# A graph network with per-node sorting: three groups of tiles instead of five, one buffer for each, and min and max as scalar_tensor_tensor

## The chip, the cores and the metric

The kernel runs on one core of a Trainium2 chip. The metric is the device time of one execution in microseconds (us); before the change it is 3176.69 us, the median of 3 runs (3176.14 to 3177.83).

## The reference, cut to what matters

Four graph layers run over x (16 graphs, 1024 nodes, 64 channels) with a sparse weighted adjacency (16 x 1024 x 1024, some 16 neighbours per node). Each layer ends in a layer norm over the residual. Layer 1 is the one that the change touches: for each node, some neighbours are dropped by a rule on their rank, and then, for each channel, three quantiles of the remaining neighbours' values are taken and summed with weights.

```python
# layer 1, for each graph; valid is the diluted adjacency > 0
vals = jnp.where(valid[..., None], x[:, None, :, :], big)
sv = jnp.sort(vals, axis=2)               # sort over the neighbours
for tau, wt in zip((0.25, 0.5, 0.75), (0.25, 0.5, 0.25)):
    pos = tau * (m - 1)                   # m valid neighbours
    agg += wt * (sv[floor(pos)] * (1 - frac) + sv[ceil(pos)] * frac)
# then x = layernorm(x + mlp(x + agg))
```

Layer 0 is one adjacency product, layer 2 is three of them with 128 channels, layer 3 is one with a threshold.

## The kernel before

**Tiling.** The 1024 nodes of a graph are ranked by their number of kept neighbours and permuted, so that each tile of 128 nodes holds nodes of like degree. `KS` gives the slots of the eight tiles: 31, 21, 19, 17, 15, 15, 13, 11. A slot holds one neighbour's row: R = 66 floats, 64 channels and 2 columns with the numbers of that neighbour's dropped partners. Tiles with like counts are sorted together, as a group (`GROUPS`): tile 0 alone with 31 slots, tiles 6 and 7 with 13, tiles 2 and 3 with 19, tiles 4 and 5 with 15, tile 1 alone with 21.

**The stages of a graph**, each a Python generator that emits a few instructions at a time:
- `words_of` (L502) reads the adjacency in 8 rows of tiles, transposes them on TensorE, makes bit words, runs layer 0 and stores the transposed adjacency to DRAM.
- `front` and `listing` (L555, L587) turn the words into neighbour lists `idx` and write the table of rows to DRAM.
- `gathered` (L808) fetches a group's rows. Each slot of 128 nodes is one indirect DMA issued by GpSimd (L815); short slots of two tiles share one through `PACKS` and `stage`. That is 129 per graph: 122 whole slots and 7 packs.
- `masked` (L847) marks dropped neighbours: VectorE finds them for one tile at a time (L862, L864), ScalarE adds a large bias to each slot (L868), and the weights `hat` of the ranks come from ScalarE (L886, L887). It needs a tile's gathers to have landed.
- `quantiles` (L891) sorts: a hand-made sorting network `NETS[n]` of min and max over whole runs of slots, each one `tensor_tensor` on VectorE (L906), between the gathered buffer `g` and a second buffer `s`.
- `summed` (L916) scales the ranks that can carry weight (`RANKS`) on ScalarE (L932), one instruction for each rank and tile, and adds them up on TensorE through an identity matrix (L936).
- `back` (L1122) does the rest of layer 1 and layers 2 and 3.

**Buffers.** All groups share four `g` buffers (tag "x", L813) and two `s` buffers (tag "y", L896), each large enough for the largest group.

**What sets the order.** Nothing is reordered by a scheduler. The loop at L1249 gives every generator a start in planned microseconds and a stretch; a heap (L1267) then emits their steps by planned time, the 16 graphs overlapping. So each engine's queue is fixed at build time, and an engine that reaches an instruction whose input is late waits there with all that stands behind it. `LENGTHS` are the planned lengths of the five sorts, 192.06 us in all for a graph; `WORDS`, `LISTS` and `BACK` stretch the other stages.

```python
add(start(q - 2), gathered(st, g), (start(q - 1) - start(q - 2)) / (many + 1))
half = (start(q) - start(q - 1)) * (PAIRS if len(GROUPS[g]) > 1 else MASKS)
add(start(q) - half, masked(st, g), 0.9 * half / (1.5 + 0.4 * count + 2.1 * len(GROUPS[g])))
add(start(q), quantiles(st, g), (start(q + 1) - start(q)) / (cost + 0.1))
add(start(q + 1) + SUMS, summed(st, g))
```

Of the kernel before, what the change touches and what calls it, by code (L numbers as in the profile page):

```python
# [10 lines left out]
F32 = mybir.dt.float32  # L11
# [9 lines left out]
P = 128  # L21
# [8 lines left out]
GROUPS = ((0,), (6, 7), (2, 3), (4, 5), (1,))  # L30
# [21 lines left out]
LENGTHS = (50.06, 35, 54.5, 19.5, 33)  # L52
WORDS, LISTS, BACK = 152.6, 133.2, 178
WORDS_STEPS, LISTS_STEPS, BACK_STEPS = 82.0, 74.0, 181.0
BEFORE = 7.874
# [10 lines left out]
RANKS = {13: (0, 9), 15: (2, 11), 19: (2, 14), 21: (3, 15), 31: (4, 23)}  # L66
# [6 lines left out]
    13: (  # L73
        "2,0,1,0,1,2,2,2,6;3,0,1,1,1,2,2,2,6;12,0,2,0,2,4,4,4,3;15,0,2,2,2,4,4,4,3;6,1,2,1,1,"
        "4,4,4,3;7,1,2,2,1,4,4,4,3;2,0,4,0,1,8,8,8,2;3,0,4,4,1,8,8,8,2;13,3,7,7,1,0,0,0,1;14,"
        "3,7,3,1,0,0,0,1;13,0,8,8,1,1,-3,-3,2;14,0,8,0,1,1,-3,1,2;13,2,6,6,1,8,6,6,2;14,2,6,2"
        ",1,8,6,8,2;12,2,4,2,1,7,6,7,2;13,2,4,4,1,7,6,6,2;11,3,5,5,1,8,7,7,2;10,3,5,3,1,8,7,8"
        ",2;8,1,2,1,1,2,2,2,3;9,1,2,2,1,2,2,2,3;2,1,9,1,2,0,0,0,1;1,1,9,9,2,0,0,0,1;5,3,11,11"
        ",2,0,0,0,1;4,3,11,3,2,0,0,0,1;3,4,8,8,3,0,0,0,1;0,4,8,4,4,0,0,0,1;11,2,4,4,1,8,8,8,1"
        ";10,2,4,2,1,8,8,8,2;2,3,5,3,1,0,0,0,1;3,3,5,5,1,0,0,0,1;6,6,8,6,2,0,0,0,1;7,6,8,8,2,"  # L80
        "0,0,0,1;12,1,2,1,1,2,2,2,5;13,1,2,2,1,2,2,2,4"
    ),
    15: (
        "3,0,1,1,1,2,2,2,7;0,0,1,0,1,2,2,2,7;3,0,2,2,1,4,4,4,4;0,0,2,0,1,4,4,4,4;13,1,3,3,1,4"
        ",4,4,3;14,1,3,1,1,4,4,4,3;12,1,2,1,1,4,4,4,4;13,1,2,2,1,4,4,4,4;3,0,4,4,3,8,8,8,2;0,"
        "0,4,0,3,8,8,8,2;3,3,7,7,1,0,0,0,1;0,3,7,3,1,0,0,0,1;6,2,4,2,2,8,8,8,2;5,2,4,4,2,8,8,"
        "8,2;5,1,2,2,1,4,4,4,4;4,1,2,1,1,4,4,4,4;8,3,4,3,1,8,8,8,2;9,3,4,4,1,8,8,8,2;2,1,9,1,"
        "6,0,0,0,1;1,0,8,8,6,0,0,0,1;8,4,8,4,4,0,0,0,1;9,4,8,8,4,0,0,0,1;11,2,4,4,2,0,0,0,1;1"
        "0,2,4,2,2,0,0,0,1;2,6,8,6,2,4,4,4,2;3,6,8,8,2,4,4,4,2;12,3,4,3,1,2,2,2,5;13,1,2,2,1,"
        "2,2,2,5"  # L90
    ),
    19: (
        "2,0,1,0,1,2,2,2,8;3,0,1,1,1,2,2,2,8;12,0,2,0,2,4,4,4,4;15,0,2,2,2,4,4,4,4;5,1,2,2,1,"
        "4,4,4,4;4,1,2,1,1,4,4,4,4;2,0,4,0,3,8,8,8,2;3,0,4,4,3,8,8,8,2;13,3,7,7,1,8,8,8,2;14,"
        "3,7,3,1,8,8,8,2;12,2,4,2,2,8,8,8,2;15,2,4,4,2,8,8,8,2;6,3,4,3,1,8,8,8,2;7,3,4,4,1,8,"
        "8,8,2;12,0,8,0,1,4,4,4,2;13,0,8,8,1,4,4,4,2;12,5,6,5,1,8,8,8,2;13,5,6,6,1,8,8,8,2;11"
        ",1,2,2,1,8,8,8,2;10,1,2,1,1,8,8,8,2;3,5,13,13,2,0,0,0,1;0,5,13,5,3,0,0,0,1;3,4,8,8,1"
        ",12,9,9,2;0,4,8,4,1,12,9,12,2;12,1,9,1,3,0,0,0,1;15,1,9,9,3,0,0,0,1;2,2,4,2,1,14,14,"
        "14,2;1,2,4,4,1,14,14,14,2;6,5,9,5,3,0,0,0,1;7,5,9,9,3,0,0,0,1;5,1,2,2,1,0,0,0,1;4,1,"
        "2,1,1,0,0,0,1;12,6,8,6,2,0,0,0,1;15,6,8,8,2,0,0,0,1;11,10,12,12,1,7,6,6,2;10,10,12,1"  # L100
        "0,1,7,6,7,2;5,0,16,16,3,0,0,0,1;4,1,17,1,2,0,0,0,1;5,3,5,5,1,4,3,3,2;4,3,5,3,1,4,3,4"
        ",2;12,9,10,9,1,2,3,2,2;13,9,10,10,1,2,3,3,2;2,8,16,8,3,0,0,0,1;3,8,16,16,3,0,0,0,1;2"
        ",3,4,3,1,2,2,2,2;3,3,4,4,1,2,2,2,2;6,11,12,11,1,2,2,2,2;7,11,12,12,1,2,2,2,2;12,4,8,"
        "4,3,8,8,8,2;13,4,8,8,3,8,8,8,2;2,2,4,2,1,4,4,4,4;3,2,4,4,1,4,4,4,3;2,7,9,7,1,0,0,0,1"
        ";3,7,9,9,1,0,0,0,1;11,3,5,5,1,8,8,8,2;10,3,5,3,1,8,8,8,2;5,1,2,2,1,0,0,0,1;12,3,4,3,"
        "1,2,2,2,6;13,3,4,4,1,2,2,2,6"
    ),
    21: (
        "2,0,1,0,1,2,2,2,8;1,0,1,1,1,2,2,2,8;13,0,2,2,1,4,4,4,4;14,0,2,0,1,4,4,4,4;3,1,3,3,1,"
        "4,4,4,4;0,1,3,1,1,4,4,4,4;2,1,2,1,1,4,4,4,4;3,1,2,2,1,4,4,4,4;12,0,4,0,4,8,8,8,2;13,"  # L110
        "0,4,4,4,8,8,8,2;2,2,4,2,2,8,8,8,2;3,2,4,4,2,8,8,8,2;5,1,2,2,1,8,8,8,2;4,1,2,1,1,8,8,"
        "8,2;12,3,4,3,1,8,8,8,2;13,3,4,4,1,8,8,8,2;8,5,6,5,1,8,8,8,2;9,5,6,6,1,8,8,8,2;3,18,1"
        "9,19,1,0,0,0,1;0,18,19,18,1,0,0,0,1;2,0,8,0,2,4,4,4,2;3,0,8,8,2,4,4,4,2;2,16,17,16,1"
        ",4,1,4,2;3,16,17,17,1,4,1,1,2;12,4,8,4,2,0,0,0,1;15,4,8,8,2,0,0,0,1;12,16,20,16,1,3,"
        "-2,3,2;15,16,20,20,1,3,-2,-2,2;2,2,10,2,2,4,4,4,2;1,2,10,10,2,4,4,4,2;11,2,4,4,2,4,6"
        ",6,2;10,2,4,2,2,4,6,4,2;11,17,19,19,1,0,0,0,1;10,17,19,17,1,0,0,0,1;12,18,20,18,1,0,"
        "0,0,1;13,18,20,20,1,0,0,0,1;12,6,8,6,2,4,4,4,2;13,6,8,8,2,4,4,4,2;12,1,2,1,1,2,2,2,2"
        ";13,1,2,2,1,2,2,2,2;11,17,18,18,1,2,2,2,2;10,17,18,17,1,2,2,2,2;9,0,16,16,1,0,0,0,1;"
        "5,1,17,17,4,0,0,0,1;4,2,18,2,3,0,0,0,1;2,7,8,7,1,2,2,2,3;3,7,8,8,1,2,2,2,3;11,8,16,1"
        "6,4,0,0,0,1;10,8,16,8,5,0,0,0,1;11,5,6,6,1,0,0,0,1;10,5,6,5,1,0,0,0,1;2,13,14,13,1,0"  # L120
# [1195 lines left out]
```

## Time and profile before

| what | value |
|---|---|
| median of 3 runs | 3176.69 us |
| span of the profiled execution, first to last instruction | 4328.2 us |
| share of its chain of waits on "another core or an unknown queue" | 28.0% |
| VectorE (DVE) busy, instructions | 2822.0 us, 6935 |
| GpSimd (POOL) busy, instructions | 2160.8 us, 2078 |
| TensorE (PE) busy, instructions | 2647.8 us, 13765 |
| ScalarE (ACT) busy, instructions | 1914.0 us, 6153 |
| the sort, L906 | 3648 instructions, 228 for each graph |
| mean granted TensorE clock | 0.764 |

The page gives no other time for the profiled execution than its span, and the span is 1151 us longer than the median of the runs. Busy time is the union of an engine's instructions. A group's row gives line, engine, operation, tiles and shapes, count, then busy us and mean ns of one, then the idle time of its engine just before such instructions and what ended it. Since the order is fixed at build time, each engine ran the same instructions in the same order in the profiled execution as in the timed ones, and only the waits between them can differ.

### The profile page before, as it was taken

The numbers are of one execution on the slowest core, as the hardware profiler recorded it, in microseconds if no ns is written. First come the engines' busy times: TensorE is split into PE (matmuls) and PEld (weight loads), VectorE is DVE, ScalarE is ACT, GpSimd is POOL, SyncE is SP. The second block draws the span as 40 slices with busy tenths as digits, with TensorE's granted clock in tenths as the row PEclk, the third lists the DMA queues.
The fourth block names the chain that finished last, engine by engine and source line by source line (L and its number), as shares of the span: only waits on it lengthen the run. The fifth ranks groups of instructions, "written<-read, shape, count | busy, mean of one in ns | idle before, by whom it ended". The sixth has DMA issues, their size and how long they took to land.

```text
span 4328.2 us, 46055 instructions
## 1 busy us (share of the span) xinstructions
PE 2647.8 (61%) x13765; PEld 1635.7 (38%) x13766; DVE 2822.0 (65%) x6935; ACT 1914.0 (44%) x6153; POOL 2160.8 (50%) x2078
## 2 busy tenths in 40 slices
PE   6034285675848567584755758476575848456478
PEld 5023152443525244352533435253343525233243
DVE  6058383865849486594857668485766859476671
ACT  2034352634536264453535455363545536253641
POOL 1715626455454645546465464546545554645600
PEclk8566597787969778796877879687787969768688
DMA  3212121322222132222213222231322222111210
GB/s 107 42 50 70 34 67 37 104 54 78 73 71 84 40 101 56 78 77 74 77 39 90 64 83 76 65 84 40 100 60 79 78 80 71 39 57 24 62 43 3
DMA packets 169056, 282.54 MB, mean 65 GB/s; under 512 B 99485, under 2 KB 102112, under 8 KB 166880
## 3 DMA queue, kind: packets, MB, share of 16 engines
q1 hardware_dynamic: 67584, 142.01, 9.9%
q0 software_dynamic: 66048, 69.88, 9.1%
q10 hardware_dynamic: 35168, 67.62, 4.1%
q8 instruction: 114, 1.87, 0.2%
q14 instruction: 142, 1.16, 0.1%
HBM read 204.33 MB, written 71.44 MB: 64 GB/s over the span
## 4 chain that ended last, share of the span: by engine, by line
another core or an unknown queue 28%; DVE 25%; PE 23%; ACT 16%; issue 7%; DMA 0%; ACTq 0%; DVEq 0%
DVE g L906 7%; PE mm L1207 7%; DVE s L906 7%; ACT g L868 6%; ACT ones_at L974 3%; PE ax L464 3%; ACT ones_at L975 2%; PE tp L439 2%; PE mm L377 2%; PE pa L936 2%; PE mm L1196 2%; ACT g L932 1%; PE mm L1141 1%; DVE top L707 1%
## 5 line engine op out<-in xcount | busy, mean ns | idle before, releaser
L815 POOL DMA_INDIRECT g<-table,idx x1952 | 2045.4, 1048 | 1919.7 <-PE pa L936 666.8
L1207 PE MATMUL mm<-adjB,msg 128*128 128x512 f32 x1536 | 769.6, 621 | 109.1 <-issue 82.4
L936 PE MATMUL pa<-g,ident 128*128 128x128 f32 (+1 forms) x1600 | 376.0, 360 | 430.1 <-ACT g L932 300.5
L868 ACT ACTIVATE g<-g,bias 128x64 f32<-128x64 f32 (+9 forms) x2272 | 596.8, 341 | 47.9 <-DVE bias L864 29.2
L906 DVE TENSOR_TENSOR s<-g 128x256 f32<-128x256 f32 (+9 forms) x944 | 531.3, 588 | 64.5 <-ACT g L868 55.5
L936 PEld LDWEIGHTS pa<-g,ident 128*128 128x128 f32 x1600 | 312.3, 248 | 574.0 <-ACT g L932 347.1
L906 DVE TENSOR_TENSOR g<-s 128x256 f32<-128x256 f32 (+8 forms) x864 | 473.4, 573 | 9.0 <-DVE s L906 3.0
L932 ACT ACTIVATE g<-g,w 128x64 f32<-128x64 f32 x1552 | 397.8, 341 | 17.2 <-DVE w L912 13.6
L1207 PEld LDWEIGHTS mm<-adjB,msg 128*128 128x128 f32 x1536 | 268.7, 197 | 301.1 <-issue 270.7
L1147 DVE TENSOR_TENSOR u<-mm,mb 128x512 f32<-128x512 f32 x32 | 22.1, 691 | 463.1 <-remote 313.5
L464 PE MATMUL ax<-at,xt 128*64 128x128 f32 x1920 | 284.5, 310 | 17.4 <-issue 17.4
L377 PE MATMUL mm<-adjB,x 128*64 128x512 f32 x512 | 272.6, 666 | 36.3 <-issue 31.3
L979 PE MATMUL mm<-ones_at,pieces 128*64 128x512 bf16 x768 | 213.0, 420 | 119.0 <-ACT ones_at L975 77.1
L464 PEld LDWEIGHTS ax<-at,xt 128*64 128x64 f32 x1920 | 250.2, 158 | 81.2 <-issue 79.1
L439 PE MATMUL tp<-ident,arow 128*128 128x128 f32 x1024 | 181.7, 309 | 156.2 <-remote 66.4
L399 DVE TENSOR_REDUCE ln_v<-sq 128x8 f32<-128x512 f32 x64 | 43.6, 681 | 296.4 <-issue 156.8
L439 PEld LDWEIGHTS tp<-ident,arow 128*128 128x128 f32 x1024 | 140.9, 162 | 205.1 <-issue 131.7
L441 ACT COPY at<-tp 128x512 f32<-128x512 f32 x240 | 139.0, 580 | 177.2 <-remote 122.3
L906 DVE TENSOR_TENSOR g<-g,s 128x256 f32<-128x256 f32 (+5 forms) x432 | 199.1, 464 | 15.1 <-remote 5.0
L906 DVE TENSOR_TENSOR g<-g 128x256 f32<-128x256 f32 (+8 forms) x304 | 200.7, 660 | 11.2 <-remote 4.0
L1219 PE MATMUL mm<-ident,tT 64*128 64x64 f32 x128 | 25.7, 295 | 293.9 <-ACT tT L380 207.4
L1210 ACT ACTIVATE hlT<-mm 128x512 f32<-128x512 f32 x96 | 57.4, 598 | 296.4 <-PE mm L1207 123.7
(225 smaller groups left out, 4361.9 us busy)
## 6 DMA issues: line engine op xcount, KB each, us to landing
arow<-in_adj_dram SPq DMA_DIRECT2D x128, 512.0 KB
adjd<-at ACTq DMA_DIRECT2D x120, 512.0 KB
adjB<-adjd SPq DMA_DIRECT2D x15, 4096.0 KB
g<-table,idx POOLq DMA_INDIRECT x1952
table<-xc ACTq DMA_DIRECT2D x16, 264.0 KB
xt<-in_x_dram SPq DMA_DIRECT2D x16, 256.0 KB
out_dram<-y SPq DMA_DIRECT2D x16, 256.0 KB
stage<-table,packed POOLq DMA_INDIRECT x112
```

What stands on the lines that cost most here:

```text
L377: nc.tensor.matmul(pa[:C, :], src[:, m, :], adjT[:, h * TH:(h + 1) * TH, m, :], start=(m == 0), stop=(m == T - 1))
L439: nc.tensor.transpose(pt[:, i * P:(i + 1) * P], a[:, j * P:(j + 1) * P], ident)
L441: nc.scalar.copy(at[:, h * TH:(h + 1) * TH, :], pt.rearrange("p (i n) -> p i n", n=P))
L464: nc.tensor.matmul(self.bank[:C, cols], self.xt[:, m + 1, :], at[:, m, :], start=(m == 0), stop=(m == T - 1))
L815: nc.gpsimd.indirect_dma_start(out=dst, out_offset=None, in_=st["table"], in_offset=bass.IndirectOffsetOnAxis(ap=index, axis=0))
L868: nc.scalar.activation(v, v, AF.Identity, bias=bias[:m, i, k:k + 1])
L906: nc.vector.tensor_tensor(box(bufs[mode >> 1 & 1], d, run, sd, count), box(bufs[mode >> 3], a, run, sa, count), box(bufs[mode >> 2 & 1], b ...
L932: nc.scalar.activation(slots(g, bufs[0], lo + r, lo + r + 1)[:, i, 0, :C], slots(g, bufs[at[r]], lo + r, lo + r + 1)[:, i, 0, :C], AF.Iden ...
L936: nc.tensor.matmul(pa[:, :(e - k) * nt * C], ident, rows_.rearrange("p (k c) -> p k c", c=R)[:, :, :C], start=(j == 0), stop=(j == len(run ...
L974: nc.scalar.activation(ones_at, iota, AF.Abs, bias=st["minus"][:, s:s + 1])
L979: nc.tensor.matmul(bank[:C, :], pieces[:, i, s, :], ones_at[:, h * HALF:(h + 1) * HALF], start=(s == 0 and i == 0), stop=False)
L1207: nc.tensor.matmul(pg, msg[:, m, :], adjT[:, h * TH:(h + 1) * TH, m, :], start=(m == 0), stop=(m == T - 1))
```

## The change

- Five groups become three: tile 0 (31 slots), tiles 4 to 7 (15 slots each), tiles 1 to 3 (21 slots each). The networks for 15 and 21 slots are new ones, those for 13 and 19 go. Smaller tiles are padded to the group's slots.
- Each group has one `g` buffer of its own (tags x0, x1, x2), and there is one `s` buffer. A group's gathers for the next graph are emitted only after its sum for this graph.
- Each min and max is a `scalar_tensor_tensor`: times 1.0, then min or max with the second tensor. Where a step has several runs (or a later step reads the columns), it takes all 66 columns of a slot as one contiguous run (`widths`), otherwise 64.
- `summed` handles ranks of three or four tiles with one matmul, 36 for each graph; ranks that a smaller tile cannot carry are left out for that tile.
- The plan has 176 us for a graph, and new constants `TURN` and `FREED`.

The networks' rows, the same renaming of tags in the fallback path, and unchanged context are cut from this diff.

```diff
-GROUPS = ((0,), (6, 7), (2, 3), (4, 5), (1,))
+GROUPS = ((0,), (4, 5, 6, 7), (1, 2, 3))
...
-LENGTHS = (50.06, 35, 54.5, 19.5, 33)
-WORDS, LISTS, BACK = 152.6, 133.2, 178
+LENGTHS = (46.0, 55.0, 75.0)
+WORDS, LISTS, BACK = 140.0, 122.0, 164.0
 WORDS_STEPS, LISTS_STEPS, BACK_STEPS = 82.0, 74.0, 181.0
-BEFORE = 7.874
+BEFORE = 8.0
+TURN = 90.0
+FREED = 20.0
...
-RANKS = {13: (0, 9), 15: (2, 11), 19: (2, 14), 21: (3, 15), 31: (4, 23)}
+RANKS = {11: (0, 9), 13: (0, 9), 15: (2, 11), 17: (2, 14), 19: (2, 14), 21: (3, 15), 31: (4, 23)}
...
+def widths(n, nt, narrow, full):
+
+    def places(buf, first, run, step, count):
+        return {(buf, first + i * step + r) for i in range(count) for r in range(run)}
+
+    read, found = set(), []
+    for mode, a, b, d, run, sa, sb, sd, count in reversed(network(n)):
+        out = places(mode >> 1 & 1, d, run, sd, count)
+        wide = bool(out & read) or (count > 1 and run * nt > 1)
+        read -= out
+        if wide:
+            read |= places(mode >> 3, a, run, sa, count) | places(mode >> 2 & 1, b, run, sb, count)
+        found.append(full if wide else narrow)
+    return found[::-1]
...
+    def room(g):
+        return len(GROUPS[g]) * max(KS[t] for t in GROUPS[g])
...
-        while "table" not in st:
+        while "table" not in st or (st["b"] and ("summed", g) not in state[st["b"] - 1]):
...
-        st["g", g] = buf = srt.tile([P, KMAX * R], F32, tag="x", name="g", bufs=4)
+        st["g", g] = buf = srt.tile([P, room(g) * R], F32, tag=f"x{g}", name="g", bufs=1)
...
-        while ("hat", g) not in st:
+        last = (st, g - 1) if g else (state[st["b"] - 1], len(GROUPS) - 1)
+        while ("hat", g) not in st or ((g or st["b"]) and ("sorted", last[1]) not in last[0]):
             yield 0.5
-        bufs = st["g", g], srt.tile([P, KMAX * R], F32, tag="y", name="s", bufs=2)
-
-        def box(buf, first, run, step, count):
+        bufs = st["g", g], srt.tile([P, room(g) * R], F32, tag="y", name="s", bufs=1)
+
+        def box(buf, first, run, step, count, width):
             v = buf[:, first * nt * R:]
-            dims = [[step * nt * R, count]] if count > 1 else []
-            dims += [[R, run * nt]] if run * nt > 1 else []
-            return bass.AP(tensor=v.tensor, offset=v.offset,
-                           ap=[list(v.ap[0])] + dims + [[1, C]])
-
-        for mode, a, b, d, run, sa, sb, sd, count in network(n):
-            nc.vector.tensor_tensor(box(bufs[mode >> 1 & 1], d, run, sd, count),
-                                    box(bufs[mode >> 3], a, run, sa, count),
-                                    box(bufs[mode >> 2 & 1], b, run, sb, count),
-                                    ALU.max if mode & 1 else ALU.min)
-            yield (nt * count * run * C + 151) / 960
+            if run * nt == 1:
+                dims = [[step * R, count]] if count > 1 else []
+                dims += [[1, width]]
+            elif width == R:
+                dims = [[step * nt * R, count]] if count > 1 else []
+                dims += [[1, run * nt * R]]
+            else:
+                dims = [[R, run * nt], [1, width]]
+            return bass.AP(tensor=v.tensor, offset=v.offset, ap=[list(v.ap[0])] + dims)
+
+        for (mode, a, b, d, run, sa, sb, sd, count), width in zip(network(n), widths(n, nt, C, R)):
+            nc.vector.scalar_tensor_tensor(box(bufs[mode >> 1 & 1], d, run, sd, count, width),
+                                           box(bufs[mode >> 3], a, run, sa, count, width), 1.0,
+                                           box(bufs[mode >> 2 & 1], b, run, sb, count, width),
+                                           op0=ALU.mult, op1=ALU.max if mode & 1 else ALU.min)
+            yield (nt * count * run * width + 151) / 960
         w = tmp.tile([P, nt, kw], F32, tag="w", name="w")
         nc.vector.tensor_reduce(w, st["hat", g].rearrange("p t s k -> p t k s"), AX.X, ALU.add)
         yield 0.2
-        st["sorted", g] = bufs, w
+        st["sorted", g] = bufs[0], w
...
-        bufs, w = st["sorted", g]
-        at = ENDS[n]
-        pa = ps.tile([P, 2 * C], F32, tag="agg", name="pa", bufs=1)
-
-        step = 2 // nt
-        runs = sorted(range(0, kw, step), key=lambda k: -max(at[k:k + step]))
-        for j, k in enumerate(sorted(runs, key=lambda k: k + step > kw)):
+        buf, w = st["sorted", g]
+        pa = ps.tile([P, max(len(x) for x in GROUPS) * C], F32, tag="agg", name="pa", bufs=1)
+
+        step = 2 if nt == 1 else 1
+        live = [[i for i, t in enumerate(tiles) if RANKS[KS[t]][0] <= lo + r <= RANKS[KS[t]][1]]
+                for r in range(kw)]
+        runs = sorted(range(0, kw, step), key=lambda k: (k + step > kw, len(live[k]) < nt))
+        for j, k in enumerate(runs):
             e = min(k + step, kw)
             for r in range(k, e):
-                for i in range(nt):
-                    nc.scalar.activation(slots(g, bufs[0], lo + r, lo + r + 1)[:, i, 0, :C],
-                                         slots(g, bufs[at[r]], lo + r, lo + r + 1)[:, i, 0, :C],
-                                         AF.Identity, scale=w[:, i, r:r + 1])
-            rows_ = bufs[0][:, (lo + k) * nt * R:(lo + e) * nt * R]
-            nc.tensor.matmul(pa[:, :(e - k) * nt * C], ident,
+                for i in live[r]:
+                    v = slots(g, buf, lo + r, lo + r + 1)[:, i, 0, :C]
+                    nc.scalar.activation(v, v, AF.Identity, scale=w[:, i, r:r + 1])
+            i0, i1 = live[k][0], live[k][-1] + 1
+            rows_ = buf[:, ((lo + k) * nt + i0) * R:((lo + e - 1) * nt + i1) * R]
+            nc.tensor.matmul(pa[:, i0 * C:((e - k - 1) * nt + i1) * C], ident,
                              rows_.rearrange("p (k c) -> p k c", c=R)[:, :, :C],
                              start=(j == 0), stop=(j == len(runs) - 1))
-            yield 0.72
+            yield 0.36 * len(live[k]) * (e - k)
+        st["summed", g] = True
...
-        ready = start(b * G - 2) - BEFORE
+        ready = start(b * G) - TURN - BEFORE
...
-            add(start(q - 2), gathered(st, g), (start(q - 1) - start(q - 2)) / (many + 1))
+            began = start(q - 2) + FREED
+            add(began, gathered(st, g), (start(q - 1) - began) / (many + 1))
```

## The prediction

> **What bounds the kernel now.** I read the page first (busy times, the chain, the costliest groups), then the instructions of the gather's line, the timeline of GpSimd beside VectorE, and busy times by stretch.
>
> The page of the kernel before:
>
> ```profile
> span 4328.2 us, 46055 instructions
> ...
> PE 2647.8 (61%) x13765; PEld 1635.7 (38%) x13766; DVE 2822.0 (65%) x6935; ACT 1914.0 (44%) x6153; POOL 2160.8 (50%) x2078
> ...
> another core or an unknown queue 28%; DVE 25%; PE 23%; ACT 16%; issue 7%; DMA 0%; ACTq 0%; DVEq 0%
> ...
> L815 POOL DMA_INDIRECT g<-table,idx x1952 | 2045.4, 1048 | 1919.7 <-PE pa L936 666.8
> ```
>
> The chain puts 28% of the span, 1212 us, on nothing that the program does. In these stretches VectorE, ScalarE and TensorE stand still while GpSimd goes on gathering. 4328 - 1212 = 3116 us, and the runs have 3177: the timed runs cannot contain these stretches. My sums are therefore made from durations of this execution without them, and anchored at 3177. One thing is hidden by them: they give GpSimd time to get ahead, so its 50% is too kind.
>
> The timeline, about one graph's bit rounds:
>
> ```profile
> 2580.05 0.95 POOL L815 DMA_INDIRECT g<-table,idx  x1 [0.30 <-issue]
> ...
> 2580.33 0.69 DVE L694 SCALAR_TENSOR_TENSOR cand<-wd,wordkey 128x512 int32<-128x512 int32 x1 [2.05 <-ACT num L689]
> ...
> 2581.30 0.95 POOL L815 DMA_INDIRECT g<-table,idx  x1 [0.30 <-issue]
> 2581.39 0.69 DVE L701 TENSOR_TENSOR wd<-wd,bit 128x512 f32<-128x512 f32 x1
> ...
> 2582.00 1.82 DVE L906 TENSOR_TENSOR s<-g 128x768 f32<-128x768 f32 x2
> 2582.55 1.22 POOL L815 DMA_INDIRECT g<-table,idx  x1 [0.30 <-issue]
> ```
>
> A gather takes 0.95 us and 0.30 more until the next, 1.25 us a step. The last one lies under `tensor_tensor` and takes 1.22. Over the whole timeline: 706 back-to-back gathers with VectorE still step at 1.251 us; 1129 with VectorE busy over 90% of the step at 1.42 us. A straight-line fit of a gather's length on what VectorE ran beside it gives 0.21 ns for each ns of `tensor_tensor`, 0.22 for `tensor_scalar`, 0.03 for `scalar_tensor_tensor`.
>
> **GpSimd's account.** In the timed runs VectorE is nearly always busy, so a step is 1.42 us and a graph's 129 gathers take 183.2 us. The gathers' line starts at 96.0 us; behind the last gather stand its mask and sort (some 32 us) and the last tail (132 us from the last sort, at 4196, to the end). 96 + 2063 x 1.41 (1.42, a little less at the two ends) + 164 = 3169 us against 3177: GpSimd alone accounts for the time.
>
> **VectorE's account.**
>
> ```profile
> core 0: us, PE busy (x) PEld busy (x) DVE busy (x) ACT busy (x) POOL busy (x), PEclk, DMA share, GB/s
> 926.00:3971.00 3045.00, 1966.90 (x10141) 1198.66 (x10142) 2102.83 (x5134) 1437.70 (x4627) 1640.05 (x1559) 0.78 0.25 69
> ```
>
> These 3045 us are 12 graphs: 175.2 us of VectorE each. Gaps under 0.4 us between its instructions, the wait of a dependent instruction for the one before, sum to 93 us, 5.8 a graph. So it needs 181.0 us of a period of about 183.2: two engines are within 1.2% of each other, and relieving one exposes the other at once.
>
> **The change, part by part**, for one graph.
>
> *Gathers.* Their number stays 129 (122 whole slots, 7 packs; padding slots are not gathered). With the sort as `scalar_tensor_tensor`, about 19 us of other `tensor_tensor` and 12 of `tensor_scalar` remain of VectorE's time; at 0.21 that is some 0.04 us a step, so 1.29 us, 166 us in all: 17 us less for GpSimd. Two rules of the Trainium skill speak against this, each stronger than what the trace supports. "SBUF — State Buffer", section "SBUF: two separate sides", lets any VectorE instruction with two SBUF inputs take the port pair shared with GpSimd; by it `scalar_tensor_tensor` would block as `tensor_tensor` does and the step stays at 1.42 (183 us). The row: 19 gathers that lie beside 376 to 665 ns of L694 or L710, both with two SBUF tensors, and almost nothing else took 943 to 952 ns, all of them. I follow the row. "Vector Engine (DVE) Microarchitecture Reference", section "Points that are easy to get wrong", says that this instruction with two SBUF sources that are not bf16 runs at half rate. The row: L694 takes 686 ns for 512 int32, L906 as `tensor_tensor` 686 for 512 f32; at half rate it would be 1219. So no change of rate; by the rule 98 us more a graph. L710 has 219 ns of fixed time instead of 153, but it has a scalar per partition, the new form a constant as L694.
>
> *The sort on VectorE.* From the networks: before, 228 instructions with 84,736 elements per partition, after, 127 with 94,472 (padding and the 2 extra columns). At 0.96 elements a ns, which L906's rows give (686 ns for 512, 420 for 256), 88.3 us become 98.4. To this comes a start-to-start cost per instruction: 68 ns where the next one is independent, 187 where it waits; over L906's pairs 112 ns on average. With fewer, longer instructions more foreign ones lie between and hide the wait, so I take 107 (bounds 93 and 131). Before 88.3 + 25.5 = 113.8, after 98.4 + 13.6 = 112.0: 1.8 us less. Two groups fewer save two sets of L870, L871, L875, L912 (0.7 us each) and one L949, 1.6 us; memsets of 8 more padding slots cost 0.55 us. Sum: 181.0 - 2.9 = 178.1 us, bounds 176 to 181.
>
> *ScalarE and TensorE.* 99 scalings as before (0.34 us each); 36 matmuls instead of 100, about 11 us less of TensorE. Neither bounds (120 and 164 us busy of 181), so I count nothing. If TensorE were the hidden limit of some stretch, this would be a gain of at most those 11 us.
>
> *One buffer for each group: the new wait.* A group's next gathers cannot start before its sum has read the buffer. Tight is the third group, tiles 1 to 3. From the end of its sort: the sum, 39 scalings in a row, 13.3 us of ScalarE, about 17 with what lies between (20 at most); 53 gathers at 1.29, 68.4 us; landing, 2 us; and the plan emits the second group's weights 1.7 us late, which moves the sorts. That is 89.1 us. The plan puts the mask of tile 3 (L862) 82.8 planned us after the sort's end (101 to the next sort, less 41.25, plus two tiles' steps), and by then VectorE has some 85 us of work from its queue: 30.7 of the first sort, 23.5 of the second, 31 of other work. It waits 4.1 us at that L862; behind it on VectorE stand the rest of the second sort and all other graphs' steps, and behind those ScalarE and TensorE. Bounds: 0 (sum in 14 us, step 1.25) and 8. Before, four shared buffers let GpSimd run two groups ahead; no row shows this wait.
>
> *First graph and end.* The second group's 52 gathers and the third's 53 come in one piece each. First gathers end at 96 + 30 = 126 us, the second group's at 192, the third's at 260; mask and weights 17 us more, so the third sort begins at 277 and ends, with 76 us of work in its stretch, at 353. Without these waits it would be some 35 us earlier. At the end, the last sum has 39 scalings instead of 13: 9 us.
>
> *Sum.* Period: 178.1 + 4.1 + half of the 2.2 us that VectorE idles now (waits on ScalarE and TensorE, not on GpSimd) = 183.3 us. Total: 353 to the end of the first graph's sorts, 14 x 183.3 = 2566, the last graph 152 (its gathers, mask and a sort with little beside it: 17 + 70 + 17 + 48), the tail 142 (132 + 9 + 1): 3213 us. The period stays what it is, for another reason, and the piecewise start adds its 35 us.
>
> **The rivals.**
> - *Faster: the loop has slack.* If sum, gathers and landing take 85 us or less, L862 never waits, and VectorE bounds: 647 + 14 x 178.1 = 3140 us. For it: 4 us decide, and ScalarE has a third of its time free. Against: TURN, FREED and the lengths leave no margin, and an in-order queue hides nothing. The border is a period of 180.7 us.
> - *The instruction holds GpSimd after all.* Step 1.42: the loop is 17 + 75.3 + 3.7 = 96 us, the wait 11, the period 190: 3307 us. Only 19 gathers speak against it, none beside L906's contiguous form.
> - *Half rate for f32.* Period about 281, 4580 us.
>
> **How the numbers follow.** No change means within 0.2%, 3170 to 3183 us, about what a measurement of this kernel can tell. The loop case has 0.58, of which 0.08 falls within 0.2%; its own range is 3160 to 3270. Faster 0.33, held GpSimd 0.07, half rate 0.02. Faster 0.33, same 0.08, slower 0.50 + 0.07 + 0.02 = 0.59. The range goes from 3110 (VectorE at its lower bound 176) to 3310.
>
> **What would show it.** Right: gathers at 1.25 to 1.30 us a step while L906 runs; L906 at 0.96 elements a ns plus 0.15 us; idle time before L862 that gathers end; L815 waiting for L936 once per group. Wrong: gathers still at 1.42 (the second rival), L906 near double (the third), or VectorE without waits at L862 (the first). A sum of the third group that takes much over 20 us would make it slower than said.

## The result and the profile after

The changed kernel takes 4211.94 us (4 runs, 4209.21 to 4222.73), the kernel before beside it 3176.41 (4 runs): 1.327 times as long, 95% interval 1.325 to 1.328. The prediction was 3213.

One thing is needed to read the later numbers. Chips differ here: on four of those that ran the experiments the kernel before takes 4466 to 4491 us, on another 3176 as where the change was measured, so kernels are compared on one chip only. What the former chips do is an experiment of its own below; the page of the kernel before, with its 4328 us, shows it too. Some executions of a kernel take over 1.5% longer than its fastest; a median called fast leaves these out.

The page of the changed kernel, in the columns of the lines shown of before:

```profile
span 4208.1 us, 42788 instructions
...
PE 2751.9 (65%) x13317; PEld 1650.6 (39%) x13318; DVE 2816.8 (67%) x5175; ACT 1909.1 (45%) x6121; POOL 2333.0 (55%) x2078
...
L797 POOL DMA_INDIRECT g<-table,idx x1952 | 2205.3, 1130 | 1592.8 <-issue 676.5
...
L844 DVE TENSOR_SCALAR hits<-g,nself 128x30 f32<-128x30 f32 (+2 forms) x128 | 32.2, 251 | 886.2 <-DMA g<-table,idx 837.6
```

VectorE is as busy as before (2817 and 2822 us), but no engine is near its span. The gather takes 1130 ns instead of 1048, and GpSimd is idle for 1593 us before its gathers; some 600 of these are the 0.30 us that lie between any two. The mask L844 (L862 in the kernel before), 32 us of work, is preceded by 886 us of idle VectorE, 838 of which end when a gather lands. The view of the waits shows the other half of the circle, GpSimd waiting for the sum's matmuls:

```profile
DVE hits L844 <- DMA g<-table,idx: 837.6, 93, 20.1
...
POOL g L797 <- PE pa L925: 526.2, 24, 29.7
```

From the fourth graph on, the gathers of the second and the third group begin 0.3 us after the last matmul of the sum that frees their buffer, in every graph.

It begins gently and grows. Two stretches of four graphs each, from the end of one graph's third sort to that of the fourth after it:

```profile
core 0: us, PE busy (x) PEld busy (x) DVE busy (x) ACT busy (x) POOL busy (x), PEclk, DMA share, GB/s
358.00:1214.00 856.00, 649.62 (x3282) 391.72 (x3283) 686.84 (x1244) 477.77 (x1545) 637.48 (x525) 0.82 0.28 78
2264.00:3344.00 1080.00, 699.09 (x3327) 419.62 (x3326) 698.24 (x1266) 479.87 (x1530) 561.27 (x516) 0.75 0.24 67
```

VectorE does the same work in both (687 and 698 us), but a graph takes 214 us in the first and 270 in the second, and GpSimd even has less to do there: its gathers take 1.09 us instead of 1.21.

### The profile page after: what moved, and what is told of

Its sections match the earlier page's. It is cut to its first block, busy times and chain, and to the rows that moved or that the text cites. A ratio compares the mean times of both kernels' runs of the same rounds, so it can differ in the third digit from the quotient of the medians.

```text
span 4208.1 us, 42788 instructions
## 1 busy us (share of the span) xinstructions
PE 2751.9 (65%) x13317; PEld 1650.6 (39%) x13318; DVE 2816.8 (67%) x5175; ACT 1909.1 (45%) x6121; POOL 2333.0 (55%) x2078
## 5 line engine op out<-in xcount | busy, mean ns | idle before, releaser
L797 POOL DMA_INDIRECT g<-table,idx x1952 | 2205.3, 1130 | 1592.8 <-issue 676.5
L850 ACT ACTIVATE g<-g,bias 128x64 f32<-128x64 f32 (+8 forms) x2272 | 616.3, 337 | 782.2 <-DVE bias L846 781.1
L925 PE MATMUL pa<-g,ident 128*128 128x128 f32 (+3 forms) x1152 | 385.7, 445 | 386.3 <-ACT g L922 384.1
L844 DVE TENSOR_SCALAR hits<-g,nself 128x30 f32<-128x30 f32 (+2 forms) x128 | 32.2, 251 | 886.2 <-DMA g<-table,idx 837.6
L894 DVE SCALAR_TENSOR_TENSOR s<-g 128x1056 f32<-128x1056 f32 (+5 forms) x448 | 481.6, 1090 | 2.2
L925 PEld LDWEIGHTS pa<-g,ident 128*128 128x128 f32 x1152 | 235.1, 249 | 592.6 <-ACT g L922 516.8
L894 DVE SCALAR_TENSOR_TENSOR g<-s 128x528 f32<-128x528 f32 (+10 forms) x368 | 375.7, 1028 | 2.1
L969 PEld LDWEIGHTS <-pieces 128*64 128x64 bf16 x768 | 100.0, 132 | 556.6 <-issue 517.8
L894 DVE SCALAR_TENSOR_TENSOR g<-g 128x990 f32<-128x990 f32 (+6 forms) x224 | 252.9, 1137 | 2.7
L894 DVE SCALAR_TENSOR_TENSOR g<-g,s 128x264 f32<-128x264 f32 (+5 forms) x336 | 247.3, 738 | 3.7
L633 PE MATMUL wd<-hi,perm 128*128 128x71 f16 x960 | 95.7, 217 | 153.7 <-DVE perm L628 153.6
```

Source lines behind the costliest of these rows:

```text
L633: nc.tensor.matmul(pw[:, :hn], ws, hi[:, t, :], start=False, stop=False)
L797: nc.gpsimd.indirect_dma_start(out=dst, out_offset=None, in_=st["table"], in_offset=bass.IndirectOffsetOnAxis(ap=index, axis=0))
L850: nc.scalar.activation(v, v, AF.Identity, bias=bias[:m, i, k:k + 1])
L894: nc.vector.scalar_tensor_tensor(box(bufs[mode >> 1 & 1], d, run, sd, count, width), box(bufs[mode >> 3], a, run, sa, count, width), 1.0, ...
L925: nc.tensor.matmul(pa[:, i0 * C:((e - k - 1) * nt + i1) * C], ident, rows_.rearrange("p (k c) -> p k c", c=R)[:, :, :C], start=(j == 0), s ...
L969: nc.tensor.matmul(bank[:C, :], pieces[:, i, s, :], ones_at[:, h * HALF:(h + 1) * HALF], start=(s == 0 and i == 0), stop=False)
```

## The experiments

**Theory and rivals after the two traces.** Theory: the plan drifts. Its `cost` counts C = 64 columns of each element, while the sort's steps now yield their true widths, mostly 66. Worked out from the networks, the three sorts take 46.88 + 56.31 + 76.82 = 180.0 planned us where 46 + 55 + 75 = 176 are planned, and each sort waits for the one before. So the sorts fall 4 planned us further behind with every graph, their sums and the gathers that wait for them too, while masks are emitted as soon as their gathers are. In the end a mask stands in VectorE's queue straight behind its gathers, ahead of the sort that would have covered them. This is reckoned from the program; the runs test it. Rivals: the loop of the single buffer alone; `scalar_tensor_tensor` holding GpSimd; different chips.

**1. The plan.** `e1_plan` and `r_plan` are the same kernel, the changed one with

```
-  cost = 0.2 + sum((len(GROUPS[g]) * x[4] * x[8] * C + 151) / 960 for x in network(n))
+  many_ = len(GROUPS[g])
+  cost = 0.2 + sum((many_ * x[4] * x[8] * w + 151) / 960
+                   for x, w in zip(network(n), widths(n, many_, C, R)))
```

`r_lag2` only puts `(C + 1)` for `C`: the three sorts then take 177.7 planned us, 1.7 too many instead of 4.0, a little under half of the error. `r_after` is the changed kernel itself.

> The changed kernel, with one line of the plan altered: the sort's planned cost counts each instruction's true width (66 or 64 columns), as its steps do, instead of always 64. Theory of the drifting plan: each graph's sorts take 180.0 planned us where 176 are meant, so they fall some 4 us further behind the other stages with every graph, until masks are queued right behind gathers that have only just been issued; the period, 211 us for the second graph and 268 from the eighth on, should then stay near 205 to 215 to the end: 3450 to 3650 us, and VectorE's idle time before its mask (886 us) should fall below 400. Rival, the single buffer for each group alone (my predicted loop, with a gather step of 1.5 us): the period of the later graphs stays above 250 and the time above 4000 us.

> The changed kernel itself, beside the kernel before on one chip, because the kernel before took 4466 us where the first four experiments ran and 3176 us where the change was measured. Theory (the emission plan drifts: 4 planned us a graph too few for the sorts): about 4212 us as measured, masks waiting for gathers 6 to 18 us each from the seventh graph on, whatever the kernel before shows; if the stretches without any engine but GpSimd are a property of the place, they come on top. Rival (the difference of 1.33 is a difference of places, not of kernels): a ratio near 1.0 to the kernel before here.

> The changed kernel with the widths that the sort really steps in counted in the plan, so that its planned lengths are 176 us and the sorts no longer fall behind. Theory (drift): the masks' waits go from some 90 us a graph to about nothing; where the kernel before takes 3176 us this one takes 3250 to 3350 (gather step 1.45 to 1.5 us under the long instructions, so 129 of them 187 to 194 us a graph), where it takes 4466 about 4440. Rival (single buffer loop, not drift): little change against the changed kernel, 4150 to 4250 us.

> The changed kernel with half of the plan's error: the sorts fall 2 planned us behind each graph instead of 4. Theory (drift): the waits at the masks begin at about twice as many graphs (period over 250 us only from graph 13 or 14 on), and the time lies nearer to the kernel with the right plan than to the changed one: 3500 to 3700 us where the kernel before takes 3176. Rival (the waits come from the loop of the single buffer alone): as the changed kernel, 4212 us.

Measured: `e1_plan` 4439 us (one run) where before takes 4466. On another chip, together, before 4483: changed 5007 (ratio 1.126, 1.115 to 1.138), the smaller error 4759 (fast 4713, two runs of four), right plan 4520 (fast 4511; ratio to before 1.012, 1.003 to 1.021). By the fast medians the first 1.7 planned us of error cost 202 us and the 2.3 above them 294: the time grows about in proportion to the error. And the mask's wait for gathers goes away with it. `r_after`:

```profile
DVE hits L844 <- DMA g<-table,idx: 484.5, 42, 20.1
```

`r_plan`, and `e1_plan` with the same line:

```profile
DVE hits L844 <- DMA g<-table,idx: 0.2, 1, 0.2
```

So the drift is shown. In `r_lag2` this wait is still 455.2 us, so it does not measure the time lost one for one. The times expected for `e1_plan` and `r_lag2` were made for the other kind of chip and missed, the first by 800 us and on the side of its rival; half the error lies in the middle, not nearer to the right plan. `r_plan` is within 2% of the 4440 us expected for this kind of chip, and `r_after` has the stretches on top of its 4212, as was allowed for. The loop of the single buffers does not go away here. In `r_plan` GpSimd still waits for sums, 898.5 us,

```profile
L797 POOL DMA_INDIRECT g<-table,idx x1952 | 2171.1, 1112 | 1991.6 <-PE pa L925 898.5
```

nearly all of it before the third group's gathers, 52 to 74 us in 13 of 15 graphs (`e1_plan`: 769.2 us). What this is worth on such a chip, where the time is within 1.2% of the kernel before, no run separates.

**2. What holds a gather.** `e2_plan_tt`: `e1_plan` with `tensor_tensor` in place of `scalar_tensor_tensor`, nothing else. `e3_plan_split`: `e1_plan` with every sort instruction cut into pieces of at most 600 elements. `b1_stt`: the kernel before with the new form of the instruction and the new widths, groups and networks as they were. `hold`: the cost by itself.

> The same with tensor_tensor instead of scalar_tensor_tensor for min and max, nothing else. Theory that a gather waits at its start for whichever VectorE instruction with two tensors is running then, to its end: both hold it alike, the mean gather stays near 1.13 to 1.2 us and the time is within 1.5% of the run before it. Rival, scalar_tensor_tensor holds GpSimd more (0.45 ns for each ns in the changed kernel's fit against 0.21 before): gathers near 1.05 us and a time lower by 3% or more. The prediction's reading, that it holds GpSimd not at all: this version slower by 5% or more.

> The first run's kernel with every min or max of more than 600 elements cut into pieces of at most 600; the same elements, more instructions. If a gather waits for the rest of the instruction that runs at its start, the wait goes with the length of one instruction: gathers' mean should fall from about 1.15 to 1.05 us, while VectorE gets some 100 instructions more for each graph at 0.07 us, 7 us. If it waits in proportion to VectorE's busy time, the mean stays. Time: 3350 to 3600, below the first run by 1 to 4% if gathers bound it, above it if VectorE does.

> The kernel before, groups, buffers and plan kept, with the change's form of min and max alone: scalar_tensor_tensor over 66 columns where needed. If it holds GpSimd as tensor_tensor does, nothing is gained, and 3% more elements cost 2.7 us of VectorE a graph: 3180 to 3240 us (ratio 1.00 to 1.02), mean gather in the profile 1.04 to 1.06 us. If it freed GpSimd as I predicted, gathers at 0.95 to 0.98 us and 3090 to 3150 us. If it held GpSimd more, 3250 or more.

> The disputed cost by itself. It computes none of the layers: blocks of 40 gathers of 128 rows of 66 floats, one behind the other, beside VectorE alone, and the input is copied to the output. Blocks: VectorE idle; tensor_tensor of 256, 1024, 2048 elements; scalar_tensor_tensor of 256, 1024, 2048; tensor_scalar of 1024; tensor_tensor with one source in PSUM, 512; then 16 loads of 512 KB through SP's queue; then 60 matmuls. Theory (the gather waits for the end of the two-tensor instruction that runs when it starts, whatever its form): step 1.25 us idle, 1.4 beside 256 elements, 1.5 to 1.7 beside 1024, 2.2 or more beside 2048, the same for both forms; 1.25 beside one SBUF source. Rival of the prediction (scalar_tensor_tensor holds nothing): 1.25 us in its three blocks. Rival (any busy VectorE slows it alike): the same step in all VectorE blocks. For the stretches in which only GpSimd works: if gathers one behind the other stop other queues, the 16 loads need far over the time that they need alone and the matmuls' instructions come late; if not, both end long before the gathers do.

Measured: `e2_plan_tt` 4480 us, 0.9% from `e1_plan` and with the same gather step where VectorE is busy over 95% of it (1.61 and 1.62 us). `b1_stt` 4513 us, ratio to before 1.012 (1.008 to 1.017): the form frees nothing. `e3_plan_split` brought that step from 1.62 to 1.51 us, but took 5026 us (one run). It has 1312 VectorE instructions more than `e1_plan`, but only 68 us more of busy time, and the stretches in which only GpSimd works grew from 688 to 974 us; why is not shown. In `hold`, GpSimd's busy time in each block of 40 gathers, in the order of the expectation (idle; `tensor_tensor` of 256, 1024, 2048; `scalar_tensor_tensor` of the same; `tensor_scalar`; one source in PSUM):

```profile
core 0: us, POOL busy (x), PEclk, DMA share, GB/s
13.20:69.60 56.40, 37.88 (x40) 0.97 0.62 198
72.20:127.20 55.00, 42.80 (x40) 0.50 0.14 24
129.20:180.40 51.20, 38.94 (x40) 0.50 0.14 26
184.90:261.50 76.60, 64.34 (x40) 0.50 0.10 17
263.40:318.40 55.00, 42.82 (x40) 0.50 0.13 24
320.30:371.50 51.20, 38.94 (x40) 0.50 0.14 26
376.00:452.60 76.60, 64.34 (x40) 0.50 0.10 17
454.50:509.10 54.60, 42.34 (x40) 0.50 0.14 24
510.90:561.00 50.10, 37.74 (x40) 0.50 0.15 26
```

Lines 2 to 4 and 5 to 7 are equal, whatever the form. While VectorE ran, a gather took 1075 ns beside 256 elements, 956 beside 1024 and 2020 beside 2048; beside `tensor_scalar` 1152, against the expectation; with one source in PSUM 944, as idle. Some lines mix in gathers that ran on after VectorE was done: beside 2048 elements it held 24 gathers and the other 16 took 944 ns, beside `tensor_scalar` 22 and 18. So the steps expected beside 256 and 2048 came, 1.38 and 2.33 us. Only the one beside 1024 was too long, because there the two rhythms fall into step: the first gather took 1683 ns, and each later one found some 0.14 us of an instruction left. In the changed kernel the timeline shows the rule (start, length):

```profile
2285.07 0.98 DVE L894 SCALAR_TENSOR_TENSOR g<-g 128x792 f32<-128x792 f32 x1
2285.27 1.61 POOL L797 DMA_INDIRECT g<-table,idx  x1 [0.31 <-issue]
...
2294.46 1.12 DVE L894 SCALAR_TENSOR_TENSOR s<-g 128x924 f32<-128x924 f32 x1
2294.81 1.59 POOL L797 DMA_INDIRECT g<-table,idx  x1 [0.30 <-issue]
...
2297.35 1.06 DVE L894 SCALAR_TENSOR_TENSOR g<-g 128x924 f32<-128x924 f32 x1
2298.03 1.18 POOL L797 DMA_INDIRECT g<-table,idx  x1 [0.39 <-DMA stage<-table,packed]
```

When these gathers start, the instruction above them still has 0.78, 0.77 and 0.38 us to run; they take 0.67, 0.65 and 0.24 us over 0.94, each time some 0.12 less than that rest. Over all gathers of this kernel the correlation of the extra time with this rest, for instructions with two tensors, is 0.91. Not every instruction holds a gather. Where one with two tensors had begun less than 0.04 us before the gather, 6 of 51 were held; where it had begun earlier and had over 0.2 us to go, 681 of 710. And 81 gathers that started under a maximum or a sum, which read one tensor, took 0.95 us on average. Longer instructions leave longer rests.

**3. The stretches in which only GpSimd works.** They sum to 718 us in the profile of the kernel before (span 4328 us; stretches over 1 us in which neither VectorE nor ScalarE nor TensorE works). The same 50 us of the first graph of the same kernel, the changed one, first where the change was measured, then as `r_after`:

```profile
q1 hardware_dynamic: 2022, 2.95, 18.4%
q0 software_dynamic: 1184, 1.25, 14.1%
q10 hardware_dynamic: 144, 0.52, 2.6%
q14 instruction: 3, 0.02, 0.2%
q8 instruction: 1, 0.02, 0.1%
```

```profile
q0 software_dynamic: 1280, 1.35, 15.7%
q14 instruction: 1, 0.01, 0.1%
```

GpSimd's gathers (q0) go on in both; in the second SP's and ScalarE's queues (q1, q10) move nothing, and of the blocks of instructions one comes instead of four. Between two gathers GpSimd leaves 0.30 us. `hold2` looks for it alone. The other kernels widen the space: behind the indirect DMA stands

```
+            for _ in range(3):
+                nc.gpsimd.memset(pause, 0.0)
```

three times (`pace`), once (`pace1`), or four times behind every fourth gather of a group (`pause4`), on a tile of 128 x 40 that nobody reads. `r_plan_` is the changed kernel with the right plan, `r_after_` the changed one, `b_` the one before.

> What else gathers one behind the other hold up. It computes none of the layers: the input is copied to the output. Six blocks, in pairs with 40 gathers and without: 80 times VectorE then ScalarE on 64 elements, each waiting for the other; 10 loads of 512 KB by SP, each waiting for a VectorE copy of the one before; 25 times a matmul, a ScalarE copy and a small VectorE instruction, each waiting for the one before. Theory A (a running gather holds up the signals between engines or the loads): the block with gathers takes well over the one without, in the worst case one step of the chain per gather, 1.25 us. Theory B (gathers alone do neither, and the stretches in which only GpSimd works need something else): pairs within some 10% of each other.

> The kernel with the right plan, and GpSimd writes a small tile three times behind each gather, so that gathers no longer follow each other after 0.30 us but after some 0.6 to 0.8. Theory (the stretches without other engines on this chip come of gathers one behind the other, and what is held gets through in the space between two): such stretches shrink from some 750 us to under 400 and the time falls from 4520 to 4100 to 4400 us, although GpSimd needs 129 x 0.4 = 50 us more a graph. Rival (the space doesn't matter): those 50 us a graph come on top wherever GpSimd bounds, 4600 to 5300 us.

> The kernel before with the same three small writes behind each gather. Theory (as for the kernel with the right plan): stretches without other engines shrink, 4000 to 4350 us instead of 4483. Rival: 4600 to 5200 us, since GpSimd's 129 steps a graph grow from 1.42 to some 1.8 us, 232 us a graph.

> The kernel before with one small write by GpSimd behind each gather instead of three: a gather is followed by the next after some 0.42 us instead of 0.30 (0.67 with three). Theory (instruction blocks are fetched only when GpSimd leaves a space): if 0.42 us are enough, 129 x (1.42 + 0.12) = 199 us a graph and 3400 to 3600 us, well under the 4003 with three writes; if not, the stretches without other engines come back and it lies between 4003 and 4483 or above.

> The changed kernel with the right plan and one small write behind each gather. Theory: as the kernel before with one write, plus some 10 us a graph for gathers that longer instructions hold longer (1.48 to 1.50 instead of 1.42 us): ratio between the two 1.03 to 1.06. Rival (the single buffers cost by themselves): ratio over 1.10, with the masks waiting for gathers although the plan is right.

> The changed kernel as it is, with one small write behind each gather. Theory (the drift costs what it cost where the change was measured, once the other stretches are away): 4250 to 4500 us, 600 us or more over the kernel with the right plan and one write. Rival (drift is worth only the 490 us that it cost here, or less): within 500 us of it.

> The kernel before with four small writes by GpSimd behind every fourth gather, the same number of writes as one behind each. Theory (a fetch needs one space now and then, long enough): as with one behind each gather or faster, 3350 to 3600 us. Rival (every gather needs a space): stretches without other engines stay, 4100 to 4500 us.

Measured, by space and time:

| kernel | space between gathers | time, us | ratio to before on that chip (95%) |
|---|---|---|---|
| `b_pace1` | 0.31 us | 4459 | 0.997 (0.994 to 0.999) |
| `r_plan_pace1` | 0.31 | 4532 | 1.008 (1.004 to 1.011) |
| `r_after_pace1` | 0.31 | 4932 | 1.104 (1.095 to 1.112) |
| `b_pace` | 0.67 | 4003 | 0.890 (0.886 to 0.893) |
| `r_plan_pace` | 0.67 | 4219 | 0.939 (0.935 to 0.942) |
| `b_pause4` | 0.30, every fourth 0.86 | 3710 | 0.827 (0.819 to 0.835) |

One write fits into the space that is there (0.31 instead of the 0.42 that I had reckoned) and changes next to nothing, so the times expected for the three `pace1` kernels missed; the drift costs 400 us there, as its rival said. A space of 0.67 us takes over half of the stretches away (718 us in the kernel before, 323 in `b_pace`), 0.86 behind every fourth gather two thirds (226 in `b_pause4`), and the times expected for the two `pace` kernels came. `b_pause4` lies between its theory and its rival.

Do gathers by themselves do it? In `hold`, on a chip where the kernel before takes 4483 us, the loads and the matmuls waited for nothing and ran beside the first block of gathers: the loads were through at 50 us, the matmuls at 62, these gathers at 69. In `hold2` loads and matmuls ran beside gathers nearly as alone (4.05 and 3.99 us from load to load). The pair of VectorE and ScalarE needed 0.51 us alone and some 0.63 beside gathers (two in each 1.25 us step), but from its 53rd turn on 1.4 us, until just after the last gather:

```profile
28.62 0.20 DVE L60 TENSOR_SCALAR small<-small 128x64 f32<-128x64 f32 x1 [0.31 <-issue]
...
29.14 0.43 DVE L60 TENSOR_SCALAR small<-small 128x64 f32<-128x64 f32 x1 [0.31 <-ACT small L61]
...
58.24 0.20 DVE L60 TENSOR_SCALAR small<-small 128x64 f32<-128x64 f32 x1 [1.17 <-ACT small L61]
...
58.61 0.94 POOL L86 DMA_INDIRECT g<-table,idx  x1 [0.30 <-issue]
59.65 0.20 DVE L60 TENSOR_SCALAR small<-small 128x64 f32<-128x64 f32 x1 [1.21 <-issue]
```

Blocks of 8 KB of instructions (q14) came at 29.8 and 35.6 us and then not before 60.2, 1.6 us after the last gather's start; 5.7 us later the pair was back at 0.51. So neither theory of `hold2` stands as written: gathers hold no signals, and what is late beside them is most likely instructions. That a late block is the cause is argued from this order in time. Gathers do not always hold a block back: two came beside these gathers, and one each beside the gathers of the later blocks (116.2 and 234.2 us). What else it takes, and why some chips show it and others do not, stays open.

**4. The shares, on a chip without the stretches** (before 3176 us). `b_pause8` has six writes behind every eighth gather of a group, a space of 1.24 us there.

> The changed kernel with the right plan and four small writes by GpSimd behind every fourth gather. Theory (what is left of the change once drift and stretches are away is some 10 us a graph of longer holds and some of the single buffers): 3750 to 3950 us, 1.01 to 1.06 times the kernel before with the same writes (3710). Rival (the single buffers cost by themselves): over 4080, 1.10 times or more, with masks that wait for gathers in most graphs.

> The changed kernel as it is, with the same writes. Theory (the drift costs what its waits at the masks say where the change was measured, 838 us, less what slack hides): 4350 to 4650 us, 600 us or more over the kernel with the right plan. Rival (the drift is worth the 490 us that it cost with the stretches, or less): within 500 us of it.

> The kernel before with six small writes behind every eighth gather, some 1.0 us of space. Theory (a fetch needs one long space now and then, and VectorE can go on for eight gathers on what it has): 3450 to 3700 us, less than with four behind every fourth, since GpSimd has fewer writes to do. Rival (spaces every 12 us are too rare): part of the stretches come back, 3750 to 4200 us.

Measured: right plan 3717 us (ratio to before 1.170, 1.167 to 1.173), changed kernel 4449 (1.402, 1.399 to 1.404), before with writes 3423 (1.078, 1.076 to 1.080). The second came as expected. The times expected of the first and the third had in part been made for the other chips, and the ratio of 1.17 is not the 1.01 to 1.06 to `b_pause4`, which ran elsewhere; `b_pause8` did not run on a chip with the stretches, so what it was to test is untested. The drift is worth 4449 - 3717 = 732 us, and VectorE's wait at the mask for gathers falls from 1082.3 to 342.9 us. The drift hardly shows at first: the second graph takes 230 us with it and 228 without, the eighth 287 and 211. With the right plan the period no longer grows (four graphs early and late, the columns as above), and of GpSimd's waits only its own pitch and the first table are left:

```profile
811.00:1670.00 859.00, 647.11 (x3332) 377.78 (x3331) 699.01 (x1267) 476.26 (x1532) 694.27 (x1029) 0.84 0.28 85
2092.00:2945.00 853.00, 650.46 (x3330) 379.95 (x3329) 698.75 (x1267) 476.09 (x1532) 687.21 (x1029) 0.84 0.28 85
```

```profile
POOL g L798 <- issue: 462.6, 1478, 1.6
POOL g L798 <- DMA table<-xc: 91.6, 1, 91.6
```

No gather waits for a sum: with the right plan and these writes the single buffers cost GpSimd nothing. The margin is small: the second group's gathers begin some 11 us after their buffer is free, the third's some 17. GpSimd simply bounds, and gathers are longer than in the kernel before:

```profile
L798 POOL DMA_INDIRECT g<-table,idx x1952 | 2309.3, 1183 | 630.1 <-issue 462.6
```

```profile
L816 POOL DMA_INDIRECT g<-table,idx x1952 | 2152.3, 1103 | 669.6 <-issue 538.2
```

The first is `r_plan_pause4`, the second `b_pause8`: 80 ns more a gather; over all 2064, those into `stage` among them, 180 us. The spaces between gathers, with the writes, sum to 65 us more, and behind the last gather come 221 us instead of 170, because the longest sort is now the last. The first gather starts 2 us earlier. Together these are the 294 us between the two.

No version beat the kernel before where it takes 3176 us. Where it takes 4480, `b_pause4` is 17% faster.

## Why the prediction was wrong, step by step

Taken without its writes, `r_plan_pause4` would take some 3410 us. This is an estimate, that kernel was not timed there: the spaces between its gathers sum to 319 us more than 0.305 us each would, and in `b_pause8`, where this excess is 254 us, the writes cost 247 (3423 - 3176). It takes for granted that no gather would wait for a sum without the writes either. No run shows that, and the writes, 20 us a graph, are longer than the margin of 11 us. From 3213 to 3410 lies mostly the wrong price of the instruction, from 3410 to 4212 the drift.

- **The period (the step that failed most).** The prediction gave every graph the same period, 183.3 us. It saw "the plan emits the second group's weights 1.7 us late" and put that into the loop as a fixed 1.7 us. It took the plan's lengths, 176 us, as given and did not add up what the steps of the new sorts yield. 4 planned us that each graph hands on to the next, since the new wait for "sorted" lets no sort catch up, grow to 64 by the last. The wait at the mask was reckoned as 4.1 us a graph; measured are 838 us at L844, 52 a graph. A graph took 214 us early and 270 late. The drift takes 732 us with the writes, some 800 without (4212 - 3410).
- **"I follow the row": gathers at 1.29 us.** They came at 1.49 (1183 + 305 ns, the writes left out), so GpSimd lost some 10 us a graph against before instead of winning 17, and it bounds: 129 gathers take 192 us where a period of 183.3 was reckoned, some 120 us over 14 graphs, and the last graph takes a whole period too instead of 152 us, some 40. The row of 19 gathers was biased: they lay beside `scalar_tensor_tensor` that started after them, by 0.28 to 0.58 us in the trace. The prediction's own timeline shows it: L694 starts at 2580.33, 0.28 us after its gather, while under the gather of 2582.55, held to 1.22 us, L906 had run since 2582.00. The fit of 0.03 asked how much of an instruction lies beside a gather, not whether it runs at its start. The trace of the kernel before had the other case as well. 30 gathers started while L694 had run for 0.04 us or more and had over 0.2 to go; they took 1.14 us on average, for example:

```profile
810.17 0.69 DVE L694 SCALAR_TENSOR_TENSOR cand<-wd,wordkey 128x512 int32<-128x512 int32 x1
810.51 1.17 POOL L815 DMA_INDIRECT g<-table,idx  x1 [0.30 <-issue]
```

  `hold` measures the hold for both forms: 1075 and 2020 ns beside 256 and 2048 elements, 944 with one source in PSUM. The Trainium skill, "SBUF — State Buffer", section "SBUF: two separate sides", was right: a VectorE instruction with two SBUF inputs that starts before a GpSimd one that reads SBUF keeps the shared pair of ports for its whole length.
- **The rival "holds GpSimd after all"** (3307 us, chance 0.07) had the mechanism for the right plan, but took 1.42 us; longer instructions made it 1.49. Its wait of 11 us at the mask came for another reason. With the writes VectorE waits 401 us at the mask (25 a graph), since GpSimd is the slower of the two, not since gathers start late behind a sum.
- **The single buffers.** With the right plan and the writes the loop did not bind; whether it would without them is open. With the drift it did, 526 us of waiting of L797 for L925, and with the right plan on the chips with the stretches (898.5 us in `r_plan`).
- **VectorE's account** held in the main: a gain of 1.8 us a graph where 2.9 were reckoned. 0.3 of it is busy time (2817 us after, 2822 before), 1.5 the gaps under 0.4 us between its instructions (70 us after, 93 before). **No half rate:** 528 elements take 0.69 to 0.71 us, 924 take 1.07 to 1.12.
- **First graph:** the third sort ends at 358 us in the changed kernel (353 said). **The tail** from the last sort to the end was right, 141 us (142 said).
- **The stretches.** To leave them out of the sum was right for this chip.

## What to carry to other kernels

Where a plan written by hand fixes the order, add up what each stage really yields against the length that the plan gives it: an error of 2% hardly shows in the first graphs and, if nothing can catch up, takes all the cushion that the queues had. Judge contention by what runs when the held instruction starts, not by how much of it lies beside; a straight-line fit over overlaps hides that. Longer VectorE instructions with two SBUF sources save starts but hold GpSimd longer, so they are no gain where GpSimd bounds.

## What the runs showed of the hardware that was not expected

- A gather that starts while VectorE runs an instruction with two SBUF sources is held for the rest of it less some 0.12 us; where the instruction had begun less than 0.04 us before, it mostly was not held (6 of 51). A source in PSUM takes the hold away (944 ns, as idle), and `tensor_scalar` of 1024 floats with one source holds as well (1152).
- On four of the five chips that ran the experiments the kernel before takes some 4480 us instead of 3176. There a space of 0.86 us behind every fourth gather gave back 17% (4478 to 3710 us), 0.31 behind each next to nothing. On another chip the same kind of writes cost 8%. Gathers alone did not stop SP's queue (`hold`: 16 loads beside 40 gathers, through before them); what stops it stays open.
